# Two-block MetaFormer forward pass: tiles of dt and dt*u copied from SBUF to SBUF, and the instruction order made in several passes

## The chip, the cores and the metric

The kernel runs on one core of a Trainium2 chip. A core has five instruction queues: PE (TensorE, matmuls), DVE (VectorE), ACT (ScalarE), POOL (GpSimd) and SP (SyncE, which in this kernel issues every DMA transfer). Each queue works in the order in which its instructions were written and waits at an instruction until the semaphores that it names have come. The metric is the device time of one execution in microseconds; the time before is the median of three runs, 3570.58 us (3565.6 to 3573.31).

## The reference

The input is x (8, 384, 32, 32). Block 0 mixes with a Mamba state space over 1024 positions, block 1 with a displacement and a small Gaussian filter for 48 positions; each is followed by a feed-forward part with binarized weights and group-wise quantization (five of the eight batch entries take part; the others are left as zeros by the quantization). The part that the change touches is the state space:

```python
xc = conv1d(xin)                       # depthwise, 3 taps
u = silu(xc)
dbc = u @ x_proj_w.T                   # dt (24), B (16), C (16)
dt = softplus(dt @ dt_proj_w.T + dt_proj_b)
A = -exp(A_log)                        # (768, 16)
def step(h, (dt_t, B_t, C_t, u_t)):
    dA = exp(dt_t[..., None] * A)
    h = dA * h + (dt_t * u_t)[..., None] * B_t[:, None, :]
    y = einsum('bdn,bn->bd', h, C_t)
y = ys + u * D
out = (y * silu(z)) @ out_proj_w.T
```

There are 768 inner channels and 16 states for each; everything is float32.

## The kernel before

**Tiling.** The sequence of each batch entry is cut in two stretches of T = 512, so there are 16 units (b, s). The 768 channels are six blocks of 128 (JC = 6), j = 0 to 5. A scan step works on one unit, one block j and one group g of states (NG = 4 groups of four states). In SBUF a tile has 128 partitions. dt and dt*u come out of softplus and of a product as soft tiles with one channel in each partition. The scan wants another layout: 32 channels (D = 32) times four states (Q = 4) fill the 128 partitions, and each quarter of 32 partitions must hold the same 32 channels. So every block of 32 channels is needed four times, once in each quarter. This is what spread does: for one soft tile it fills two dts (or dus) tiles of [128, 2, 512], tile p with channel blocks 2p and 2p+1, four copies of each.

**prep and spread.** prep makes two blocks at a time: PE forms dt (L873), ACT applies softplus (L883), POOL multiplies by u (L896), and spread is called for dt (into dts) and for dt*u (into dus). A spread first writes the soft tile to a DRAM tile via (256 KB) and then issues eight reads of it, each into 32 partitions of a dts or dus tile with two channel blocks (128 KB). There are 192 spreads. The rings are: soft three slots, via twelve, dts four, dus four.

**scan.** For each (unit, j, g) and each half p: POOL multiplies dus by B (L927), ACT takes exp of dts times A twice (L937), DVE runs the recurrence with two scans (L952). For half 0 POOL multiplies by C (L973), for half 1 DVE does (L986). The last states are kept by POOL (L969) and ACT (L979). PE sums over states into y (L994). t tiles have five slots, and PE's sum gives them back. B and C reach the partitions through bc tiles, read from DRAM (bcd).

**Beside it.** The same queues carry the input and output projections (L704, L1056), the feed-forward parts (L1445 and L1524 on PE, L1457 and L1536 on ACT, gelu L1500 on ACT, clips on POOL), layer norms, and the displacement. Their weights come in by DMA for each use (w<-w1d, w<-w2d, win, wo).

**What sets the order.** Every instruction is first recorded as an Op with an engine, a supposed duration and a key (a place in the order, counted in scan steps). Flow.run then plays through a list schedule: at each moment a free engine takes, among its instructions whose inputs are there and whose tile slots are free, the one with the lowest key. The keys are shifted by pseudo-random amounts: DRAWS has one seed for each 25 us of planned time, and shift turns it into a shift by instruction (ONE) and by engine and kind (ALL). PEN is added to the key of an ACT instruction that needs another function table. SP is taken to issue in 0.38 us with at most eight transfers in flight (LANES), and the semaphores of its transfers are eight as well: every transfer waits for the eighth before it. The instructions are emitted in the order in which this play took them. So a change of one transfer's size or number changes the order of all five queues.

Of the kernel before, what the change touches and what calls it, by code (L numbers as in the profile page):

```python
# [17 lines left out]
P = 128  # L18
B, C, HW = 8, 384, 1024
T = 512  # L20
# [6 lines left out]
Q = 4  # L27
D = P // Q
# [21 lines left out]
PEN = 8.61  # L50
# [38 lines left out]

STEP = 25.0
DRAWS = [
    2588809238, 452375479, 3182300674, 892127437, 3031607106, 4190915799, 210801287, 2528267595,
    1456515859, 0, 3667191977, 1777003549, 0, 289602391, 2360043521, 2893761654,
    1734824177, 2595276797, 1859152535, 420106053, 3187747945, 3121993781, 3537900339, 3781817979,
    1783676794, 500156423, 1014657074, 812403421, 2779270353, 2511900677, 4161990074, 2234806154,
    3075364087, 332485381, 1936396653, 2423255391, 3223520118, 2106840927, 1194216589, 154361651,
    1325576476, 2228588731, 1746166578, 1393485667, 3298820094, 2167670678, 0, 1658737982,
    2077953505, 2037467793, 1520888315, 1581728111, 3672070717, 3354909891, 1803808393, 4150367721,  # L100
    3281395725, 1519460387, 901569797, 618278083, 3122266317, 2079668595, 1489438893, 4286922582,
    1437111022, 872287307, 1167138051, 0, 1838008287, 3016755925, 3498114163, 3916969487,
    180074838, 64412836, 507811054, 1600843621, 25363757, 0, 682985741, 3258605221,
    1225562961, 0, 2191594738, 2731506639, 0, 2590361159, 2105546166, 1917697076,
    2936522859, 449918706, 807634013, 1769699081, 4123052838, 3422563802, 2854028781, 3998098897,
    1351550483, 2957050150, 3108490381, 0, 3870246271, 3129552247, 4423401, 1585339085,
    2919941273, 2106441706, 2263314457, 1450830237, 318771235, 2472105454, 2452787799, 3820223235,
    1566145129, 2085494553, 835678459, 1114623705, 693252553, 4024613474, 833387989, 3847970403,
    1743556437, 2448629961, 1025051962, 888405083, 4144082655, 1523794525, 2137060207, 1893166927,
    3205541950, 693684995, 2577056702, 4001291010, 934710037, 2114703579, 3848563781, 3766732577,  # L110
]
ONE, ALL = (0.0, 2.0, 6.0, 16.0), (0.0, 6.0, 20.0, 60.0)
ENGS = ("PE", "DVE", "ACT", "POOL", "SP")


# [7 lines left out]
def drawn(a, b):  # L123
    return mixed((mixed(a) + b) & 0xFFFFFFFF) / 4294967296.0 - 0.5


def shift(seed, o):
    if not seed:
        return 0.0
    v = 0.0  # L130
    if seed & 3:
        v += ONE[seed & 3] * drawn(seed, o.n + 100)
    if seed >> 2 & 3:
        v += ALL[seed >> 2 & 3] * drawn(seed, ENGS.index(o.eng) + 5 * o.kind)
    return v


# [42 lines left out]


class Op:
    __slots__ = ("eng", "us", "lag", "fn", "bufs", "key", "n", "wait", "next", "table", "at", "ready", "kind")


SETS = {
# [10 lines left out]
TIE = 0  # L197
# [5 lines left out]
class Flow:  # L203
# [89 lines left out]
            last = ends[o.n]  # L293
        return fills

    def run(self):
        nc = self.nc
        waiting = {e: [] for e in self.on}
        busy = {e: 0.0 for e in self.on}
        table, now, out = None, 0.0, []  # L300
# [4 lines left out]
        ends = {}  # L305
        left = len(self.ops)
        step = 0
        draw = lambda k: DRAWS[k] if k < len(DRAWS) else 0

        def enter(o):  # L310

            new = {}
            for b in o.bufs:
                if b.slot is None and b.ring.ordered:
                    k = new[b.ring] = new.get(b.ring, 0) + 1
                    if b.n > b.ring.given + k - 1:
                        b.ring.turn.setdefault(b.n - k + 1, []).append(o)
                        return
            insort(waiting[o.eng], (o.key + shift(draw(step), o), o.n, o))

        for o in self.ops:
            if o.wait == 0:
# [2 lines left out]
        while left:  # L325
            if int(now / STEP) != step:
                step = int(now / STEP)
                for q in waiting.values():
                    q[:] = sorted((o.key + shift(draw(step), o), n, o) for _, n, o in q)
            while done and done[0][0] <= now + 1e-9:  # L330
                _, _, o = heapq.heappop(done)
                for p in o.next:
                    p.wait -= 1
                    if p.wait == 0:
                        p.ready = now
                        enter(p)
                for b in o.bufs:
                    b.left -= 1
                    if b.left == 0:
                        b.ring.free.append(b.slot)  # L340
                        b.end = now
            moved = False
            nexts = []
            for e, q in waiting.items():
                if busy[e] > now + 1e-9:
                    continue
                best = None
                for i, (k, n, o) in enumerate(q):
                    if best is not None and (k > best[0] or TIE and k == best[0]):
                        break  # L350
                    if o.table is not None and o.table != table:
                        t = o.ready + (self.HOLD[o.table] if o.key > RUSH else 0.0)
                        if now < t - 1e-9:
                            nexts.append(t)
                            continue
                        k += PEN
                        if best is not None and k >= best[0]:
                            continue
                    if e == "SP" and landed[-LANES] > now + 1e-9:
                        nexts.append(landed[-LANES])  # L360
                        break
                    if Ring.open(o.bufs):
                        best = (k, i)
                if best is None:
                    continue
                o = q.pop(best[1])[2]
                for b in o.bufs:
                    if b.slot is None:
                        b.slot = b.ring.free.pop(0)
                        b.ring.given += 1  # L370
                        for p in b.ring.turn.pop(b.ring.given, ()):
                            enter(p)
                us = o.us
                if o.table is not None and o.table != table:
                    us += self.SWITCH
                    table = o.table
                if e == "PE":
                    if now - idle >= IDLE:
                        cold = now + COLD
                    if now < cold - 1e-9:  # L380
                        us *= 2
                    if o.us > 0.5:
                        idle = now + us
                busy[e] = now + us
                if e == "SP":
                    dma_free = max(dma_free, now) + (o.lag - 1.8)
                    end = max(dma_free, now + us) + 1.8
                    landed.append(end)
                else:
                    end = now + us + o.lag  # L390
                heapq.heappush(done, (end, o.n, o))
                o.at = now
                if e == "PE":
                    ends[o.n] = now + us
                    for b in o.bufs:
                        b.at = min(b.at, now)
                out.append(o)
                left -= 1
                moved = True
            if moved:  # L400
                continue
            t = [x for x in busy.values() if x > now + 1e-9] + nexts
            if done:
                t.append(done[0][0])
            t = [x for x in t if x > now + 1e-9]
            assert t, "the instructions that are left wait for one another"
            now = min(t)
        self.end = now
        fills = self.gaps(out, ends) if self.filler else {}
        table = None  # L410
        out.sort(key=lambda o: o is not self.lead)
# [9 lines left out]
def metaformer_flow(ctx, tc, x, mw, f0, offset, f1, out):  # L421
# [77 lines left out]
    lt_r = ring("lt", [P, 4, P], 3)  # L499
    sm_r = ring("sm", [P, 16], 8, ordered=False)  # L500
    bcd_r = ring("bcd", [2 * N, T], 2, dr)
    via_r = ring("via", [P, T], 12, dr)
    hd_r = ring("hd", [NS * MC // 2, P, 2, T], 2, dr)
    x1 = [one(f"x1_{b}", [C, HW], NS * KC, dr) for b in range(B)]
    x2 = [one(f"x2_{b}", [C, HW], NS * KC, dr) for b in range(GS)]
# [339 lines left out]

    def spread(src, r):

        via = via_r.new()
        dma(lambda: via.ap, lambda: src.ap, [src], [via])
        dst = [r.new(Q), r.new(Q)]  # L850
        for p in range(2):
            for q in range(Q):
                dma(
                    lambda p=p, q=q: dst[p].ap[q * D : (q + 1) * D],
                    lambda p=p: via.ap.rearrange("(c d) t -> d c t", d=D)[:, 2 * p : 2 * p + 2, :],
                    [via],
                    [dst[p][q]],
                    128,
                )
        return dst  # L860

# [960 lines left out]
```

## Time and profile before

| What | Value |
|---|---|
| median of the runs, three of them | 3570.58 us |
| the profiled execution, its own time | 3572.66 us |
| its span | 3570.9 us |
| instructions in the profile | 35,878 |
| mean granted TensorE clock | 0.934 |
| bytes moved by DMA | 777.44 MB, 218 GB/s |
| share of the span in which the 16 DMA engines were busy | 75.4% |
| reads of via into dts and into dus | 768 and 768, of 128 KB |
| writes of via | 192, of 256 KB |
| SP's time from issue to landing, all transfers | 1.6 / 4.4 / 11.0 us (min / median / max) |

The busy share of an engine is an average over the whole span. An engine's idle time is put down to what ended it, and matmuls are pipelined, so a busy PE is not a PE at its peak. PEld is the loading of weights into the array, which overlaps with matmuls. A transfer's time to landing counts from SP's issue to the semaphore. The chain of waits is the sequence of work that ended last, followed back from the last instruction.

### The profile page before, as it was taken

What the parts mean: (1) busy time and instruction counts of PE and PEld (TensorE: products, weight loads), DVE (VectorE), ACT (ScalarE), POOL (GpSimd) and SP (SyncE); (2) the same over time, 40 slices, a digit from 0 to 9 for tenths busy, and PEclk for the clock granted to TensorE, in tenths of its full rate; (3) what the DMA queues carried; (4) which work ended last, traced back from release to release, by engine and by line L of the source; (5) the groups of instructions that cost most, each with busy time, mean ns of one, the idle gap of its engine ahead of it and who ended that gap; (6) DMA issues with size and microseconds to landing.
All of it is one profiled execution on the core that took longest, in us unless ns stands there. A gap on an engine that the chain in (4) does not pass through costs nothing.

```text
span 3570.9 us, 35878 instructions
## 1 busy us (share of the span) xinstructions
PE 3120.2 (87%) x9620; PEld 1136.4 (32%) x9620; DVE 3086.1 (86%) x3080; ACT 2469.2 (69%) x3641; POOL 3155.6 (88%) x1680
## 2 busy tenths in 40 slices
PE   5788888888899997899999789999878999877997
PEld 2222323223233332333333233333223333323334
DVE  2898988789887989998988999988898998889985
ACT  4777877757677686686768667777666777766561
POOL 3889999898797899889899997999989899998893
PEclk7888989998899998999999999999988999888999
DMA  6768768696775987769597686868777897977955
GB/s 156 185 185 229 213 199 224 176 249 183 222 221 166 271 243 205 203 200 253 178 270 235 180 233 213 247 193 265 228 205 241 237 254 224 275 209 221 267 171 178
DMA packets 680819, 777.44 MB, mean 218 GB/s; under 512 B 113688, under 2 KB 434088, under 8 KB 680616
## 3 DMA queue, kind: packets, MB, share of 16 engines
q1 hardware_dynamic: 680616, 775.14, 75.4%
q8 instruction: 77, 1.26, 0.2%
q14 instruction: 126, 1.03, 0.1%
HBM read 578.45 MB, written 196.48 MB: 217 GB/s over the span
## 4 chain that ended last, share of the span: by engine, by line
PE 37%; DVE 20%; DMA 12%; POOL 12%; ACT 10%; issue 7%; SPq 2%; POOLq 0%; DVEq 0%; ACTq 0%
PE mm L1445 11%; PE mm L1524 8%; POOL t L927 7%; DVE dp L952 6%; PE mm L704 5%; DVE t L952 5%; PE y L994 4%; PE mm L1056 4%; DVE t L986 3%; POOL t L973 2%; DMA dts<-via 2%; ACT L417 2%; ACT dp L937 2%; SPq L268 2%; DMA dus<-via 2%
## 5 line engine op out<-in xcount | busy, mean ns | idle before, releaser
L927 POOL TENSOR_TENSOR t<-dus,bc 128x1024 f32<-128x1024 f32 x768 | 1798.6, 2361 | 154.1 <-PE y L994 112.7
L973 POOL TENSOR_TENSOR t<-t,bc 128x1024 f32<-128x1024 f32 x384 | 905.6, 2361 | 57.1 <-DVE t L952 48.6
L1524 PE MATMUL mm<-hb,w 128*128 128x512 f32 x1440 | 679.6, 610 | 35.3 <-ACT hb L1500 15.5
L937 ACT ACTIVATE da<-dts,aneg 128x512 f32<-128x512 f32 x768 | 521.2, 685 | 254.4 <-DVE t L952 227.3
L1445 PE MATMUL mm<-tn,w 128*128 128x512 f32 x1440 | 663.1, 605 | 23.8 <-DMA w<-w1d 5.3
L937 ACT ACTIVATE dp<-dts,aneg 128x512 f32<-128x512 f32 x768 | 528.1, 688 | 182.5 <-DVE t L986 170.4
L994 PE MATMUL y<-t,sel 128*32 128x512 f32 x3072 | 531.4, 652 | 140.0 <-POOL t L973 79.6
L952 DVE TENSOR_TENSOR_SCAN dp<-dp,h,t 128x512 f32<-128x512 f32 x384 | 491.4, 1280 | 52.3 <-ACT dp L937 42.0
L952 DVE TENSOR_TENSOR_SCAN dp<-dp,t 128x512 f32<-128x512 f32 x384 | 468.4, 1220 | 69.9 <-ACT dp L937 49.2
L952 DVE TENSOR_TENSOR_SCAN t<-da,h,t 128x512 f32<-128x512 f32 x384 | 482.6, 1268 | 52.1 <-POOL t L927 45.5
L952 DVE TENSOR_TENSOR_SCAN t<-da,t 128x512 f32<-128x512 f32 x384 | 458.9, 1208 | 72.0 <-POOL t L927 58.7
L417 ACT ACT_TABLE_LOAD x372 | 477.3, 1283 | 6.2
L704 PE MATMUL mm<-xn,win 128*128 128x512 f32 x900 | 438.6, 629 | 42.0 <-DVE xn L595 9.9
L986 DVE TENSOR_TENSOR t<-dp,bc 128x1024 f32<-128x1024 f32 x384 | 465.9, 1213 | 8.2 <-ACT h L979 2.5
L1524 PEld LDWEIGHTS mm<-hb,w 128*128 128x128 f32 x1440 | 263.2, 192 | 441.5 <-issue 350.4
L1445 PEld LDWEIGHTS mm<-tn,w 128*128 128x128 f32 x1440 | 267.1, 192 | 409.8 <-issue 303.7
L1056 PE MATMUL mm<-z,wo 128*128 128x512 f32 x552 | 273.4, 626 | 5.9 <-DMA wo<-in_L_conv_out_proj_w 2.9
L704 PEld LDWEIGHTS mm<-xn,win 128*128 128x128 f32 x900 | 172.5, 199 | 293.1 <-issue 205.3
L1457 ACT ACTIVATE he<-mm,b 128x512 f32<-128x512 f32 x240 | 162.9, 680 | 126.0 <-PE mm L1445 124.9
L994 PEld LDWEIGHTS y<-t,sel 128*32 128x32 f32 x3072 | 80.1, 112 | 498.2 <-issue 168.9
L542 PE MATMUL mm<-sq,pick 96*128 96x512 f32 x208 | 129.7, 709 | 42.4 <-ACT sq L535 39.2
L1056 PEld LDWEIGHTS mm<-z,wo 128*128 128x128 f32 x552 | 103.6, 198 | 164.4 <-issue 143.5
(135 smaller groups left out, 3076.7 us busy)
## 6 DMA issues: line engine op xcount, KB each, us to landing
dts<-via SPq DMA_DIRECT2D x768, 128.0 KB, 4.0
dus<-via SPq DMA_DIRECT2D x768, 128.0 KB, 4.3
hd<-he SPq DMA_DIRECT2D x120, 512.0 KB, 4.7
hb<-hd SPq DMA_DIRECT2D x120, 512.0 KB, 5.8
via<-soft SPq DMA_DIRECT2D x192, 256.0 KB, 3.9
w<-w2d SPq DMA_DIRECT2D x120, 384.0 KB, 4.4
w<-w1d SPq DMA_DIRECT2D x240, 192.0 KB, 4.0
bc<-bcd SPq DMA_DIRECT2D x256, 128.0 KB, 5.0
```

The lines of the kernel that those rows point to most:

```text
L417: nc.scalar.preload_act_table_set(SETS[table])
L704: e.matmul(acc.ap, w.ap[:, k, :], xn.ap[:, k, :], start=(k == 0), stop=(k == KC - 1))
L927: lambda e, t=t, du=du: e.tensor_mul(t.ap, du.ap, wide(0)),
L937: lambda e, c=c, r=r, dt=dt: e.activation(decay(c), dt.ap[:, r, :], AF.Exp, scale=aneg.ap[:, j * Q + c, g : g + 1],),
L952: e.tensor_tensor_scan(t.ap[:, r, :] if p == 0 else decay(c), decay(c), t.ap[:, r, :], 0.0 if s == 0 else hst[j][p].ap[:, g, r : r + 1], A ...
L973: op("POOL", 2.35, lambda e, t=t: e.tensor_mul(t.ap, t.ap, wide(1)), [bc], [t])
L986: lambda e, t=t: e.tensor_mul(t.ap, da[2].ap, wide(1)),
L994: e.matmul(y.ap[c * D : (c + 1) * D, :], sel.ap, ts[c // 2].ap[:, c % 2, :], start=(g == 0), stop=(g == NG - 1), tile_position=(0, c * D),)
L1056: e.matmul(o.ap, flat()[:, j, :], zs[j].ap, start=(j == 0), stop=(j == JC - 1))
L1445: e.matmul(acc.ap, w.ap[:, k, :], tn.ap[:, k, :], start=(k == 0), stop=(k == KC - 1),)
L1457: lambda e, he=he, r=r, m=m, acc=acc: e.activation(he.ap[:, r, :], acc.ap, AF.Identity, bias=b1.ap[:, m : m + 1]),
L1524: e.matmul(acc.ap, w.ap[:, part * 2 + r, :], hs[m // 2].ap[:, r * T : (r + 1) * T], start=(m == 0), stop=(m == MC - 1),)
```

## The change

spread no longer goes through DRAM. It issues sixteen copies from the soft tile: for each of the four channel blocks c and each quarter q, 32 partitions of the soft tile go to 32 partitions of dts or dus (64 KB). A dts or dus tile now has eight parts, each written by its own copy. The ring via is gone.

The order is played through eight times instead of once. The first play uses the keys as before, with new seeds; every later play ranks an instruction by the time at which the play before it started it (divided by PACE), with seeds of its own and smaller shifts. The last play's order is emitted. Other constants (ROWS, CONVS, the K values, PEN, GBS) stay as they are.

```diff
-STEP = 25.0
+STEP, PACE = 25.0, 9.06
 DRAWS = [
...
 ]
-ONE, ALL = (0.0, 2.0, 6.0, 16.0), (0.0, 6.0, 20.0, 60.0)
+ONE = ((0.0, 2.0, 6.0, 16.0), (0.0, 0.3, 1.0, 3.0))
+ALL = ((0.0, 6.0, 20.0, 60.0), (0.0, 1.0, 4.0, 12.0))
...
-def shift(seed, o):
+def shift(seed, o, later):
...
-        v += ONE[seed & 3] * drawn(seed, o.n + 100)
+        v += ONE[later][seed & 3] * drawn(seed, o.n + 100)
     if seed >> 2 & 3:
-        v += ALL[seed >> 2 & 3] * drawn(seed, ENGS.index(o.eng) + 5 * o.kind)
+        v += ALL[later][seed >> 2 & 3] * drawn(seed, ENGS.index(o.eng) + 5 * o.kind)
...
-    def run(self):
-        nc = self.nc
+    def arrange(self, k):
+
+        draws = DRAWS[k]
...
-            insort(waiting[o.eng], (o.key + shift(draw(step), o), o.n, o))
+            insort(waiting[o.eng], (o.rank + shift(draw(step), o, k > 0), o.n, o))
...
         self.end = now
+        return out, ends
+
+    def run(self):
+        nc = self.nc
+        bufs = {b for o in self.ops for b in o.bufs}
+        for o in self.ops:
+            o.rank = o.key
+        for k in range(len(DRAWS)):
+            waits, lefts = [o.wait for o in self.ops], [(b, b.left) for b in bufs]
+            frees = [(r, list(r.free)) for r in {b.ring for b in bufs}]
+            out, ends = self.arrange(k)
+            if k + 1 == len(DRAWS):
+                break
+            for o, w in zip(self.ops, waits):
+                o.rank, o.wait = o.at / PACE, w
+            for b, left in lefts:
+                b.left, b.slot, b.at, b.end = left, None, 1e9, 1e9
+            for r, free in frees:
+                r.free, r.given, r.turn = free, 0, {}
         fills = self.gaps(out, ends) if self.filler else {}
...
-    via_r = ring("via", [P, T], 12, dr)
...
     def spread(src, r):
 
-        via = via_r.new()
-        dma(lambda: via.ap, lambda: src.ap, [src], [via])
-        dst = [r.new(Q), r.new(Q)]
-        for p in range(2):
+        dst = [r.new(2 * Q), r.new(2 * Q)]
+        for c in range(Q):
             for q in range(Q):
                 dma(
-                    lambda p=p, q=q: dst[p].ap[q * D : (q + 1) * D],
-                    lambda p=p: via.ap.rearrange("(c d) t -> d c t", d=D)[:, 2 * p : 2 * p + 2, :],
-                    [via],
-                    [dst[p][q]],
-                    128,
+                    lambda c=c, q=q: dst[c // 2].ap[q * D : (q + 1) * D, c % 2, :],
+                    lambda c=c: src.ap[c * D : (c + 1) * D, :],
+                    [src],
+                    [dst[c // 2][q * 2 + c % 2]],
+                    64,
                 )
         return dst
```

## The prediction

> **What bounds the kernel now.** I read the busy shares first, then the same three engines by stage.
>
> ```profile
> PE 3120.2 (87%) x9620; PEld 1136.4 (32%) x9620; DVE 3086.1 (86%) x3080; ACT 2469.2 (69%) x3641; POOL 3155.6 (88%) x1680
> ```
> ```profile
> 0.00:100.00 100.00, 61.76 (x162) 26.30 (x163) 33.16 (x39) 49.46 (x78) 41.04 (x44) 0.73 0.67 160
> 100.00:3450.00 3350.00, 2958.91 (x9097) 1061.53 (x9096) 2976.30 (x2949) 2377.36 (x3510) 3054.36 (x1608) 0.94 0.77 221
> 3450.00:3571.00 121.00, 99.50 (x363) 48.58 (x361) 76.64 (x95) 42.42 (x53) 60.17 (x29) 0.95 0.55 179
> ```
>
> The columns of the second fence are the stretch, its length, busy time of PE, PEld, DVE, ACT and POOL, the granted clock, the DMA share and GB/s. No engine is alone at its limit: PE, DVE and POOL stand within two points of each other, and in the middle stretch POOL, the fullest, still idles 3350.0 - 3054.4 = 295.6 us. That idle time, plus a start and an end in which the pipeline fills and drains, is all that transfers and order can win without less work. Next: who ends it.
>
> ```profile
> POOL t L927 <- PE y L994: 112.7, 72, 6.2
> POOL h L969 <- DVE t L952: 60.6, 28, 6.3
> POOL t L973 <- DVE t L952: 48.6, 21, 6.0
> POOL t L927 <- DMA dus<-via: 6.5, 3, 5.1
> ```
>
> (us in total, times, longest.) POOL mostly waits for a free t tile, which PE's sum at L994 gives back, and for DVE's scans. The transfers that the change rebuilds end 6.5 us of it. Over all engines, the tile view of via lists 33.0 us of waits on its transfers (its ten rows added); the largest are these.
>
> ```profile
>   ACT da L937: 14.0, 6
>   POOL t L927: 7.4, 4
> ```
>
> The chain of waits sees more of them. Adding all of its pieces by name, dts<-via has 17 pieces with 72.6 us, dus<-via 14 with 59.3, via<-soft 5 with 18.9: 150.8 us, 4% of the span. A typical place, start and length in us:
>
> ```profile
> 1801.03 3.79 DMA dts<-via
> 1804.84 4.53 DMA dus<-via
> 1809.38 4.19 DMA dts<-via
> ```
>
> The pieces follow one another on SP's queue: each is released by an earlier transfer, not by compute. The chain steps through whatever came last, so its share is an upper figure and the engines' own idle time (33.0 us) a lower one.
>
> **The change, part by part.** Prices of transfers, from issues (KB, median us to landing) and from SP's own line (ns min/median/max):
>
> ```profile
> dts<-via SPq DMA_DIRECT2D x768, 128.0 KB, 4.0
> via<-soft SPq DMA_DIRECT2D x192, 256.0 KB, 3.9
> bcd<-dbc SPq DMA_DIRECT2D x16, 64.0 KB, 2.8
> ```
> ```profile
> L268 SPq DMA_DIRECT2D dts<-via x768: 302/425/1665, 62.1 to 3430.4; - x192
> L268 SPq DMA_DIRECT2D bcd<-dbc x16: 332/338/532, 51.6 to 3226.4; - x16
> ```
>
> *Transfers.* There are 192 spreads (16 units, 6 channel blocks, dt and dt*u). Each had one 256 KB write and eight 128 KB reads; it now has sixteen 64 KB copies. Bytes fall from 192 x 1.25 MiB to 192 x 1 MiB. No row shows SBUF to SBUF; the nearest is the 64 KB bcd<-dbc, 2.8 us, and I take that (the other end is 4.0, the landing of today's reads). Delivery of one dt alone: today 0.37 + 3.9 + 8 x 0.425 + 4.0 = 11.7 us; then 16 x 0.338 + 2.8 = 8.2. For dt and dt*u together: today 2 x 0.37 + 3.9 + 16 x 0.425 + 4.0 = 15.4; then 32 x 0.338 + 2.8 = 13.6. So the leg through DRAM goes, but most of it is paid back in issues. On the chain this would be 18.9 us of via and 31 pieces x (131.9/31 - 2.8) = 45 us, together -64. By the engines' idle time it is at most -33. I take -33, because engines at 87% refill what one queue gives back; the ends are -64 and, if landing stays at 4.0 us, -10 (about half of the via pieces, as other queue work takes their place). What is late next is POOL's wait for t tiles (112.7 us), which this part does not touch.
>
> *SP's queue.* It issues 3,434 transfers now and 4,778 in the changed kernel's order: +1344, at 0.338 us = 454 us of queue time. Its 1928 us of waits (all rows of SP's own list added) are the cover: it is an in-order queue that mostly waits for a slot to come free. Of the 3,434 issues, 197 pieces with 66.8 us lie on the chain; the same share of the new ones is 66.8 x 1344/3434 x 0.338/0.425 = +21 us. Behind them stand the weight loads (w<-w1d, w<-w2d, win), for which PE's L1445, L1524 and L704 wait, the hd writes and reads of the FFN, and bc<-bcd for POOL. If the cover is gone it costs up to 454 us. Every transfer waits for the eighth before it: at 2.8 us to landing that passes one each 0.35 us, no tighter than the issue itself; at 4.0 it passes one each 0.5 us.
>
> *Waits per reader.* A half of dts or dus is now written by eight copies instead of four. In the two orders, waits on transfers grow from 892 to 1,349 on ACT and from 1,016 to 1,360 on POOL; each that does not fit the instruction is a semaphore instruction of 38 to 42 ns (medians at L937 and L927). That is up to 344 x 0.042 = +14 us on POOL. The page puts POOLq and ACTq at 0% of the chain, so I take +4; ends 0 and +14. Behind such a wait on ACT stand the FFN's evictions (L1457, L1536), and behind those PE's mm slots.
>
> *The soft tile* is held until sixteen copies have landed, 8.2 us instead of 0.37 + 3.9. Three slots serve four tiles of a prep, so the fourth (POOL L896) waits for the first one's copies. I cost it at nothing: a channel block lasts 3571/96 = 37 us, and L896 waited 0.5 us in all for via. Without this cover it would be 48 preps x 3.9 = 187 us. The DRAM ring's twelve parking places, which let a block be prepared before its dts slot is free, go as well; the same 37 us cover that.
>
> *The order.* All five queues are listed anew, every DMA of SP's and every compute instruction included; their numbers of instructions are the same but for SP's and for ACT's table loads, 376 in the listing of before and 353 in that of after.
>
> ```profile
> L417 ACT ACT_TABLE_LOAD x372 | 477.3, 1283 | 6.2
> ```
>
> That is 23 x 1.283 = 29.5 us less on ACT, which idles 973 us in the middle stretch. On the chain are 54 loads with 64.5 us, 14%; so -5 us (ends 0 and -29.5). What the rest of a new order is worth no row shows. Its stake is POOL's 295.6 us; I take the same 6% by which the loads fall, -18 us, and as ends a third of the stake won (-98) and a fifth lost (+59).
>
> Sum: -33 + 21 + 4 - 5 - 18 = -31. From the profiled span 3570.9, that gives 3540 us; span and median of the runs (3570.58) agree to 0.3 us, so nothing is added.
>
> A rule speaks against the first part. The row first: with 32-partition writes, dts<-via leaves each 0.425 us, 131 KB / 0.425 = 308 GB/s, because transfers overlap. The Trainium skill, "SBUF — State Buffer", section "Summary: rules for kernel authors", asks for 128 partitions and one transfer rather than several; "DMA: Bandwidth & Descriptors", section "Measured (HBM→SBUF, 128 partitions, SWDGE, issued from GpSimd)", puts a lone 64 KB transfer at 138 GB/s. By that rate an estimate is 201 MB / 138 GB/s = 1459 us for the spreads alone, and the sum would go to the slower rival. The row already goes past such a rate, so I stay with it.
>
> **The rivals.**
>
> *SP's queue becomes the bound (slower).* Place: the burst of a block, 32 copies where 18 stood, in front of weight loads. Price: 454 us of added queue time times the uncovered share. With the other terms at -52 (33 + 5 + 18 - 4), it decides from 52/454 = 11% uncovered, against the 5% (21 us) that I take. At 20% it is +91 - 52 = +39: 3610 us. For it: the queue's waits and its issues (3434 x about 0.4 = 1370 us) already fill 3300 us of the span, so there is no empty time, only waits that can shrink. Against it: most of SP's waits are for slots of weights whose readers hardly wait for them (PE L1445 waits 5.3 us for w<-w1d).
>
> *The order is worth much more (faster).* A third of POOL's idle time instead of 6%: 3540 - 80 = 3460 us. For it: 112.7 us of POOL's waits are for PE's L994, which an order can place earlier. Against it: three engines at 87% jam one another whichever goes first.
>
> *Hidden anyway (no change).* Transfers hide behind compute, and the order gives and takes: 3571 us. For it: only 33 us of engine waits name these transfers. Against it: all five queues differ from the first rows on, and a tie is unlikely.
>
> **How the numbers follow.** My forecast near 3540 has 0.43, the stronger gain 0.15, no change 0.07, the bound queue 0.35. No change means within 0.2%, 7 us, about what a measurement of this kernel can tell; its runs span 3565.6 to 3573.3. So faster 0.58, same 0.07, slower 0.35. The forecast's own range is 3507 (transfers at -64) to 3563 (transfers at -10). For 8 in 10 it reaches down to the stronger gain, 3460, and up past the slower rival, to 3620 (22% uncovered); 0.08 is left below and 0.12 above.
>
> **What would show it.** Right: dts<-soft lands in about 2.8 us with an issue near 0.34; ACT's and POOL's waits on dts and dus under 20 us; SP's waits shrink by about 400 us while PE's waits on w<-w1d, w<-w2d and win grow by under 20; table loads near 350; POOL's idle time in the middle near 265 us. Wrong: landing at 4 us or issues over 0.4 us, weight loads among the first releasers of PE, or POOL's idle time above 300 us for reasons of order (L994, L952) with the transfers in time.

## The result and the profile after

The changed kernel takes 3993.65 us (median of four runs, 3988.5 to 3996.92) against 3570.05 us for the kernel before: ratio 1.118, 95% interval 1.116 to 1.120. It is slower by 424 us. The prediction, 3540 us, had the wrong sign, and its range ended at 3620.

The page's busy line and the middle stretch of the changed kernel (stretch, length, busy time of PE, PEld, DVE, ACT, POOL, granted clock, DMA share, GB/s):

```profile
PE 3225.1 (81%) x9620; PEld 1171.2 (29%) x9620; DVE 3094.7 (78%) x3080; ACT 2440.1 (61%) x3618; POOL 3156.0 (79%) x1680
```
```profile
100.00:3850.00 3750.00, 3056.13 (x9048) 1096.20 (x9046) 2955.96 (x2924) 2339.64 (x3473) 3028.03 (x1596) 0.90 0.63 184
```

POOL and DVE do the same work as before (3155.6 and 3086.1 us then) in a longer span; PE's is 105 us longer at a lower granted clock (0.895 over the span, 0.934 before). In the later runs the clock is lower where the time is longer, whatever slowed the kernel (0.937 at 3520 us in half_copies; 0.900 at 3905 us in stale_before, which has the old transfers); what part of the 424 us it adds was not separated. POOL idles 3750.0 - 3028.0 = 722 us in the middle, against 296 before. DMA is not what filled up: its share fell from 0.77 to 0.63. The waits of the changed kernel (us in total, times, longest) show where it waits now:

```profile
POOL t L1071 <- PE y L1138: 314.1, 123, 11.1
PE mm L1589 <- DMA w<-w1d: 90.6, 33, 9.3
PE mm L1668 <- DMA w<-w2d: 70.2, 25, 7.6
ACT da L1081 <- DMA dts<-soft: 67.1, 16, 10.8
POOL soft L1040 <- DMA dts<-soft: 66.7, 15, 16.4
PE mm L850 <- DMA win<-in_L_conv_in_proj_w: 65.7, 21, 7.9
```

(L1071, L1138, L1589, L1668, L1081, L1040 and L850 are L927, L994, L1445, L1524, L937, L896 and L704 of before.) Weight loads, which PE hardly waited for, now stop it; the same rows before:

```profile
PE mm L704 <- DMA win<-in_L_conv_in_proj_w: 8.5, 5, 2.7
PE mm L1524 <- DMA w<-w2d: 7.5, 7, 2.1
PE mm L1445 <- DMA w<-w1d: 5.3, 7, 1.6
```

POOL's largest wait, 314 us, is for the t slots that PE's sum gives back (112.7 us before). Adding all rows whose releaser is a transfer, PE's idle time behind transfers rose from 61 to 384 us, POOL's from 44 to 276, ACT's from 30 to 117, DVE's from 38 to 100. Yet the transfers themselves land sooner than before (KB, median us to landing):

```profile
dts<-soft SPq DMA_DIRECT2D x1536, 64.0 KB, 2.2
dus<-soft SPq DMA_DIRECT2D x1536, 64.0 KB, 2.1
```

The weight loads land sooner too (w<-w1d 3.3 us, 4.0 before). So the transfers are late at their start. SP's own line in the changed kernel (ns, min/median/max):

```profile
L395 SPq DMA_DIRECT2D dts<-soft x1536: 507/588/3821, 53.1 to 3881.6; - x192
L395 SPq DMA_DIRECT2D dus<-soft x1536: 507/588/2199, 55.8 to 3880.4; - x192
L395 SPq DMA_DIRECT2D w<-w1d x240: 359/488/2055, 486.6 to 3803.4; - x120
```

A copy from SBUF to SBUF holds SP for 588 ns, where the prediction had 338. Loads issued among them cost more as well: w<-w1d has 488 ns, 376 before. SP's waits add up to 1140 us, 1928 before. What is not wait is 3992 - 1140 = 2852 us, against 3571 - 1928 = 1643: SP's work grew by about 1210 us. The lengths of SP's transfer issues, added up over the trace, say the same: 2660 us, 1469 before. A stretch of SP's timeline in the changed kernel (start, length in us) shows how a weight load gets lost in it:

```profile
2015.01 0.51 SPq L395 DMA_DIRECT2D dts<-soft  x1
2015.62 0.54 SPq L395 DMA_DIRECT2D w<-w2d  x1
2016.21 3.74 SPq L395 DMA_DIRECT2D dts<-soft  x6
2020.05 0.53 SPq L395 DMA_DIRECT2D w<-w1d  x1
2020.62 1.79 SPq L395 DMA_DIRECT2D dts<-soft  x3
2022.51 1.00 SPq L395 DMA_DIRECT2D bc<-bcd  x2
2023.56 1.78 SPq L395 DMA_DIRECT2D dts<-soft  x3
2025.44 6.87 SPq L395 DMA_DIRECT2D dus<-soft  x11
...
2066.48 1.84 SPq L395 DMA_DIRECT2D w<-w1d  x2
```

From 2015 to 2068 us SP has hardly a gap. Between the load of w1d at 2020.05 and the next at 2066.48 it issues 53 copies and 16 loads of bc, and no weights. PE does one load's worth of L1589 (six matmuls) in 2.7 us. After 2032 us it runs none, until the next load has landed (in brackets the idle time before, and what ended it):

```profile
2071.38 4.54 PE L1589 MATMUL mm<-tn,w 128*128 128x512 f32 x5 [9.32 <-DMA w<-w1d]
```

### The profile page after: what moved, and what is told of

Same layout as the page of the kernel before. It is cut to its first block, busy times and chain, and to the rows that moved or that the text cites. A ratio compares the mean times of both kernels' runs of the same rounds, so it can differ in the third digit from the quotient of the medians.

```text
span 3992.2 us, 37566 instructions
## 1 busy us (share of the span) xinstructions
PE 3225.1 (81%) x9620; PEld 1171.2 (29%) x9620; DVE 3094.7 (78%) x3080; ACT 2440.1 (61%) x3618; POOL 3156.0 (79%) x1680
## 5 line engine op out<-in xcount | busy, mean ns | idle before, releaser
L1071 POOL TENSOR_TENSOR t<-dus,bc 128x1024 f32<-128x1024 f32 x768 | 1797.3, 2357 | 423.0 <-PE y L1138 314.1
L1589 PE MATMUL mm<-tn,w 128*128 128x512 f32 x1440 | 714.0, 640 | 113.7 <-DMA w<-w1d 90.6
L1668 PE MATMUL mm<-hb,w 128*128 128x512 f32 x1440 | 708.3, 632 | 87.3 <-DMA w<-w2d 70.2
L1081 ACT ACTIVATE da<-dts,aneg 128x512 f32<-128x512 f32 x768 | 522.8, 685 | 353.4 <-DVE t L1096 277.6
L1081 ACT ACTIVATE dp<-dts,aneg 128x512 f32<-128x512 f32 x768 | 527.6, 687 | 183.0 <-DVE t L1130 153.4
L1138 PE MATMUL y<-t,sel 128*32 128x512 f32 x3072 | 517.4, 647 | 135.2 <-POOL t L1117 68.0
L850 PE MATMUL mm<-xn,win 128*128 128x512 f32 x900 | 445.4, 637 | 92.3 <-DMA win<-in_L_conv_in_proj_w 65.7
L1589 PEld LDWEIGHTS mm<-tn,w 128*128 128x128 f32 x1440 | 279.1, 202 | 537.2 <-issue 390.9
L1668 PEld LDWEIGHTS mm<-hb,w 128*128 128x128 f32 x1440 | 274.1, 199 | 509.9 <-issue 383.0
L1200 PE MATMUL mm<-z,wo 128*128 128x512 f32 x552 | 290.4, 663 | 40.7 <-DMA wo<-in_L_conv_out_proj_w 31.7
L850 PEld LDWEIGHTS mm<-xn,win 128*128 128x128 f32 x900 | 176.0, 202 | 348.6 <-issue 235.6
L1040 POOL TENSOR_TENSOR soft<-soft,u 128x512 f32<-128x512 f32 x96 | 121.9, 1270 | 153.0 <-DMA dts<-soft 66.7
L1138 PEld LDWEIGHTS y<-t,sel 128*32 128x32 f32 x3072 | 77.3, 112 | 483.1 <-issue 205.4
L1611 DVE TENSOR_REDUCE sm<-he 128x1 f32<-128x1024 f32 x120 | 144.4, 1204 | 66.4 <-ACT he L1601 64.8
```

The lines of the kernel that those rows point to most:

```text
L850: e.matmul(acc.ap, w.ap[:, k, :], xn.ap[:, k, :], start=(k == 0), stop=(k == KC - 1))
L1071: lambda e, t=t, du=du: e.tensor_mul(t.ap, du.ap, wide(0)),
L1081: lambda e, c=c, r=r, dt=dt: e.activation(decay(c), dt.ap[:, r, :], AF.Exp, scale=aneg.ap[:, j * Q + c, g : g + 1],),
L1138: e.matmul(y.ap[c * D : (c + 1) * D, :], sel.ap, ts[c // 2].ap[:, c % 2, :], start=(g == 0), stop=(g == NG - 1), tile_position=(0, c * D),)
L1200: e.matmul(o.ap, flat()[:, j, :], zs[j].ap, start=(j == 0), stop=(j == JC - 1))
L1589: e.matmul(acc.ap, w.ap[:, k, :], tn.ap[:, k, :], start=(k == 0), stop=(k == KC - 1),)
```

## The experiments

Theory A: the issue of these copies fills SP's queue. Theory B: the eight-pass order is at fault. Theory C: 64 KB transfers of 32 partitions move slowly.

**The price by itself.** The kernel issue_prices has SP issue 32 transfers of each of twelve shapes, nothing else on the chip:

```diff
+group("aa", cut(0, 32, T), own(0, 32, T), [128, T])             # SBUF to SBUF, 32 rows of 2 KB
+group("ai", cut(0, 32, T), lambda: x[0][0:32, :T], [128, T])    # DRAM to SBUF, the same shape
+group("ak", cut(0, 32, T), own(0, 32, T), [128, T], dr)         # SBUF to DRAM, the same shape
...
```

> Leaves out all of the computation: SP issues 32 transfers of each of twelve shapes, one shape after the other, with nothing else on the chip, and the output is filled from one tile. Theory A1 (the issue of a copy from SBUF to SBUF of 32 partitions costs SP 0.5 to 0.6 us by itself): aa and ab 0.5 to 0.6 us, a read from DRAM (ai) and a write to DRAM (ak) of the same shape 0.30 to 0.35. Theory A2 (the price comes from contention with the kernel's other transfers): aa and ab 0.30 to 0.40 us like ai and ak. If the price goes with the rows, ad (128 partitions) is far above aa and ag (16) below; if with the bytes, af (4 KB rows) is above aa and ae (512 B rows) below.

The tile view of the groups in issue_prices (ns, min/median/max; first and last start):

```profile
L25 SPq DMA_DIRECT2D aa<-src x32: 578/589/603, 3.0 to 22.7; - x32
...
L25 SPq DMA_DIRECT2D ad<-src x32: 598/630/652, 64.5 to 85.2; - x32
...
L25 SPq DMA_DIRECT2D ae<-src x32: 588/589/632, 85.9 to 105.6; - x32
...
L25 SPq DMA_DIRECT2D af<-src x32: 588/590/663, 106.2 to 126.3; - x32
...
L25 SPq DMA_DIRECT2D ag<-src x32: 507/587/735, 127.0 to 147.0; - x32
...
L25 SPq DMA_DIRECT2D ai<-in_x x32: 419/419/724, 168.5 to 183.4; - x32
...
L25 SPq DMA_DIRECT2D ak<-src x32: 302/422/540, 207.7 to 223.7; - x32
```

A1 is right about the copies: 589 ns on an idle chip, with no contention. With both ends in SBUF the price is nearly the same whatever is moved: 16 KB (ae), 64 KB (aa), 128 KB (af) and 256 KB (ad, 128 partitions, 630 ns), 16 rows instead of 32 (ag), aligned or shifted partitions (ab, 589 ns) all cost about the same. With one end in DRAM, 32 rows cost 419 to 422 in a row of such transfers, so the expected 300 to 350 was missed. It was met where the issues did not follow close on one another. The same view of parts of two groups (aj reads 128 rows from DRAM):

```profile
L25 SPq DMA_DIRECT2D aj<-in_x x10: 422/430/652, 183.8 to 188.3; - x10
L25 SPq DMA_DIRECT2D aj<-in_x x22: 327/328/373, 190.5 to 207.1; - x22
L25 SPq DMA_DIRECT2D ak<-src x7: 302/302/332, 207.7 to 211.6; - x7
```

The ten of the first line start every 0.5 us, one right behind another; the 22 of the second have pauses of at least 0.27 us before them, in which SP waits for a landing, and so have the seven of ak. So the price depends on the two ends, and on whether a transfer is issued right behind another. Sixteen small copies pay sixteen prices, where one larger copy would pay one.

**Half the bytes, half the count.** All three kernels keep the changed kernel's order on PE, DVE, ACT and POOL. From the ninth spread on, half_bytes moves only the first 256 columns of each copy; half_copies leaves out the copies for two of the four quarters, and twelve_copies those for one. What is not copied stays at old values.

```diff
+W = T if len(made) <= 8 else T // 2          # half_bytes
-lambda c=c: src.ap[c * D : (c + 1) * D, :],
+lambda c=c, W=W: src.ap[c * D : (c + 1) * D, :W],
...
+if q >= 2 and not full:                      # half_copies; q >= 3 in twelve_copies
+    o.fn = lambda e: None
```

> The changed kernel in its own order; from the ninth spread on each of the sixteen copies moves half of its columns (32 KB), so dt and dt*u are wrong in the other half. Theory A (the issue sets the time, and its price does not go with the bytes): issue stays 0.59 us and the time within 1.5% of the changed kernel, 3930 to 4050 us. Theory C (transfers of 32 partitions are slow to move): half of 200 MB less, under 3850 us.

> The changed kernel in its own order on PE, DVE, ACT and POOL; from the ninth spread on eight of its sixteen copies are not issued, so the upper half of the partitions of dts and dus holds old values. Same copy size, half the count: SP has 1,472 issues of 0.59 us less, 868 us. Theory A: 3500 to 3700 us, most of the loss gone. Theory B (the order itself is at fault): above 3850 us.

> As half_copies, but twelve of the sixteen copies are issued (the last quarter of the partitions holds old values). The plan reserved 16 x 0.38 = 6.1 us of SP for a spread; eight copies take 4.7, twelve 7.1, sixteen 9.4. Theory A, with a loss that starts where the real time passes the reserved one: 3600 to 3760 us, above the straight half of the way's lower side. If the loss were a plain sum in copies, half of the way between 3520 and 3993: 3757 us.

half_bytes took 3968 us (ratio 1.110, 1.103 to 1.117): with half the bytes nothing but 25 us goes, as theory A had it and against theory C. half_copies took 3520 us (ratio 0.985, 0.979 to 0.991), 474 us less than the changed kernel and under the kernel before: against theory B. Its waits for transfers are back near the old ones (PE 73 us, POOL 50; 61 and 44 before). Its busy line:

```profile
PE 3096.6 (88%) x9620; PEld 1134.3 (32%) x9620; DVE 3082.6 (88%) x3080; ACT 2438.2 (69%) x3618; POOL 3156.8 (90%) x1680
```

twelve_copies took 3637 us (ratio 1.019, 1.016 to 1.021). The first four copies more cost 117 us, the next four 357. The list schedule reserved 16 x 0.38 = 6.1 us of SP for a spread; eight copies take 8 x 0.588 = 4.7, twelve 7.1, sixteen 9.4. The loss grows faster than the count, as theory A has it (a plain sum would have given 3757). Three points don't tell where it starts, nor whether the reserved time or a full queue sets that place.

**The same transfers, cheaper to issue.** copies_from_dram keeps number, size and destination of the copies but reads the matrix w_in in DRAM, so dt and dt*u are those numbers, and a soft tile is free without waiting for copies.

```diff
-lambda c=c: src.ap[c * D : (c + 1) * D, :],
+lambda c=c: w_in[c * D : (c + 1) * D, :T],
```

> The changed kernel in its own order; the sixteen transfers of each spread keep number, size and destination but read a matrix in DRAM instead of the soft tile, so dt and dt*u are wrong, and a soft tile is free without waiting for them. Issue falls from 0.59 to 0.42 us by the price list, 3072 x 0.17 = 520 us of SP's time. Theory A: 3600 to 3830 us. Theory C (32 partitions, 64 KB): above 3930 us. The wait for soft tiles (136 us in the changed kernel) goes too, so a fall of up to 136 us alone would speak for that hold.

It took 3637 us (ratio 1.017, 1.011 to 1.023), 357 us less than the changed kernel. SP's line in copies_from_dram:

```profile
L395 SPq DMA_DIRECT2D dts<-in_L_conv_in_proj_w x1536: 310/419/2999, 53.1 to 3520.6; - x192
```

588 - 419 = 169 ns on 3,072 issues are 519 us of SP's time. The soft tiles, whose hold made POOL's L1040 wait 122 us for copies in the changed kernel, are freed by the same edit, and their hold was not tried alone. But twelve_copies, where the hold is left in, takes the same 3637 us with about the same work on SP. Five kernels have the changed kernel's order on the four engines and copies without a leg through DRAM; sorted by SP's work (span less SP's waits, in us) they are sorted by time, whatever the copies' number, size and source:

| Kernel | SP's work | Time |
|---|---|---|
| half_copies | 1873 | 3520 |
| copies_from_dram | 2324 | 3637 |
| twelve_copies | 2362 | 3637 |
| half_bytes | 2841 | 3968 |
| the changed kernel | 2852 | 3994 |

**The order.** Four kernels take spread and order apart. The no_seeds pair has one pass and all seeds zero, through DRAM and direct:

```diff
-DRAWS = [
...
+DRAWS = [0]
```

> The kernel before with all seeds zero: one pass, order by the keys alone. This is the base for no_seeds_direct, so that neither kernel has seeds that fit it. Both theories expect it slower than before, by 2 to 10%: 3640 to 3930 us.

> The same with the direct spread, nothing else: one pass, all seeds zero. Theory A: 300 to 500 us above no_seeds_via, with issues of 0.59 us. Theory B: within 100 us of it.

They took 3693 us (as expected) and 4313 us: the direct spread alone costs 620 us in an order fitted to neither, more than the 300 to 500 of theory A, and its PE waits 438 us behind transfers (68 in the other). Then the changed kernel's passes with the old spread put back, its control, and the passes without seeds:

```diff
 DRAWS = [ ... ]                              # via_new_order: the eight lists as they are
+via_r = ring("via", [P, T], 12, dr)
...
-v += ONE[seed & 3] * drawn(seed, o.n + 100)  # stale_before: the kernel before
+v += ONE[seed & 3] * drawn(seed, o.n + 101)
...
+DRAWS = [[0]] * 8                            # no_seeds_via_eight
```

> The changed kernel with the spread through DRAM put back (one 256 KB write and eight 128 KB reads), the order still made in eight passes; the seeds were drawn for another number of instructions, so some of their fit is lost. Theory A (SP's queue: a copy from SBUF to SBUF takes SP 588 ns to issue, so 3,072 of them fill it): 3560 to 3640 us, issue of dts<-via near 0.43 us, SP's waits back near 1900 us. Theory B (the eight-pass order is itself bad): 3850 to 4000 us.

> The kernel before with its seeds drawn for other instructions (the number of each is shifted by one); nothing else. It is the control for via_new_order, whose seeds had lost their fit too. If lost fit explains its 3948 us, this one is far above no_seeds_via: 3750 to 3950 us. If the eight passes explain it, this one stays at 3650 to 3720.

> The spread through DRAM, eight passes, all seeds zero: against no_seeds_via (3693 us, one pass) it shows what the passes do without seeds. If repeated passes improve the order by themselves: 3550 to 3670 us. If they do nothing: 3670 to 3730. If they spoil it: above 3750.

via_new_order took 3948 us (ratio 1.105), where theory A had 3560 to 3640. Most of that is not the passes: stale_before, the old kernel with seeds that fall on the wrong instructions, took 3905 us (ratio 1.094), 212 us above no seeds at all. Passes without seeds gave 3744 us, 50 us above one pass and between the expectations for doing nothing and for harm. In these two kernels seeds that have lost their list of instructions do harm. So the time of via_new_order says nothing about theory A. Its waits do: its PE waits 78 us behind transfers, against 384 in the changed kernel at nearly the same time.

**The planner.** planner_told corrects the plan's price of a copy:

```diff
-def dma(self, dst, src, reads=(), writes=(), kb=256.0):
+def dma(self, dst, src, reads=(), writes=(), kb=256.0, us=0.38):
...
                     64,
+                    0.59,
```

> The changed kernel with one constant of the list schedule corrected: a copy from SBUF to SBUF keeps SP for 0.59 us instead of 0.38. The seeds stay, so they fit less. Theory A1 (the work on SP is too much wherever it is put): 3850 to 4050 us. Theory A2 (the loss comes from a plan that did not know the price): under 3750 us.

It took 4334 us (ratio 1.212), outside both expectations, and near no_seeds_direct. That its seeds had lost their fit too is likely and not shown. Whether a plan that knows the price and has seeds found for it could hide the copies stays open.

**The old transfers in the new order.** These three compute everything and keep the changed kernel's list of instructions, and so its order on the four engines. The sixteen places of a spread on SP carry one write to DRAM and eight reads of 128 KB. In via_in_its_slots each read stands at the second of its two places; in reads_later and reads_latest it is put on the queue at least 4 or 8 planned us after the write (or right ahead of the first instruction that needs it).

```diff
+if not seen:
+    e.dma_start(via, src.ap)
+if (p, q) in seen:
+    e.dma_start(dst[p].ap[q * D : (q + 1) * D], via.rearrange(...)[:, 2 * p : 2 * p + 2, :])
+seen.add((p, q))
...
+fl.pending.append((wrote[0] + LATER, dst[p], read))     # LATER 4.0 or 8.0
```

> The changed kernel with the order of PE, DVE, ACT and POOL exactly as it is; only on SP the sixteen copies of a spread become, at their own places, one write of the soft tile to DRAM and eight reads of 128 KB, each at the second of the two places that it stands for. SP's spread costs 0.37 + 8 x 0.42 = 3.8 us instead of 16 x 0.59 = 9.4, but SP waits for the write to land before the first read. Theory A (SP's issue is the whole loss, the new order is better than the old): 3500 to 3580 us, at or under the kernel before. Theory B (the new order is no better): 3580 to 3700 us.

> As via_in_its_slots, but a read of the DRAM tile is put on SP's queue no sooner than 4 planned us after its write (or right ahead of the first instruction that needs it). SP then issues other transfers while the write lands. If SP's stand of 490 us made the 3643 us: 3490 to 3560 us, under the kernel before, SP's waits for via under 200 us. If the order is no better than the old one: 3580 to 3650 us.

> The same with 8 planned us. SP's waits for via under 50 us. If the stand made the time: 3480 to 3560 us, at or under reads_later, unless the later reads make ACT and POOL wait for dts and dus (then above reads_later). If the order: 3580 to 3650 us.

via_in_its_slots took 3643 us (ratio 1.020, 1.018 to 1.022): 351 us of the 424 come back, but the time lies in theory B's range (an order no better than the old one) and above theory A's. SP's wait for the write in it (its largest), in reads_later and in reads_latest:

```profile
SPq L1005 <- DMA via<-soft: 489.9, 165, 6.9
```
```profile
SPq L1016 <- DMA via<-soft: 258.9, 111, 6.7
```
```profile
SPq L1016 <- DMA via<-soft: 63.8, 36, 5.6
```

reads_later took 3574 us (ratio 1.001, 0.9997 to 1.0023), reads_latest 3584 us (1.004, 1.002 to 1.005). With SP's stand before unlanded writes halved, 69 of the 73 us over the kernel before are gone, so it made most of them. But the hoped-for 3490 to 3560 was missed: taking away more of the stand did not go below the kernel before, and with 8 us other work waits (ACT da on dts<-via 29.7 us against 23.5 with 4 us, POOL t on bc<-bcd 30.3 against 17.1). So with the transfers of before, the new order takes the time of the old one, and the direct copies make the loss of 420 us. A gain from the order does not show. None that computes everything beats the kernel before.

## Why the prediction was wrong

**The step that failed is SP's price.** The prediction took the issue of a copy from the row of bcd<-dbc, 0.338 us, because it is the nearest in size; it is a write to DRAM, and the price goes with the two ends, not with the bytes. The 3,072 copies cost 3072 x 0.588 = 1806 us of SP where the 1,728 old transfers cost 1536 x 0.425 + 192 x 0.372 = 724: +1082 us, not +454. With the dearer issue of the loads between them SP's work grew by about 1210 us. The prediction also priced only the 1,344 added issues, though all 3,072 are of the new kind. And the row's median was no bound: 13 of its sixteen issues came after a pause, and ak shows 302 ns for such ones against 422 in a row. That error is the smaller one: at 422 ns the copies would have cost 3072 x 0.422 - 724 = +572 us.

**The mechanism of the slower rival was right, its size was not.** "SP's queue becomes the bound" had the place (a block's burst in front of weight loads), the sign that would show it (weight loads among PE's first releasers) and the condition (more than 11% uncovered). Its price was 454 us, of which 20% gave 3610. Measured, about 424 of 1210 us are uncovered, 35% (taking the other terms as nothing, as none of their gains shows). It was right that SP's queue has "no empty time, only waits that can shrink": the waits shrank by 788 us, and the rest became span. Two of its own signs of being wrong came: issues over 0.4 us, and weight loads among the first releasers of PE. (The lower end of its range, 3507, is a slip: 3540 less 31 is 3509.)

**Transfers (-33).** They land in 2.1 to 2.2 us, sooner than the 2.8 assumed, and the leg through DRAM is gone. It won nothing, as the queue ahead of them grew: ACT waits 86 us for dts and POOL's L1071 43 us for dus, not under 20.

**The soft tile, costed at nothing.** The cover was a block's 37 us. It failed with SP: POOL's L1040 waited 153 us in all, 122 of them for copies of a soft tile. A copy's tile is held for about 16 x 0.588 + 2.1 = 11.5 us even if nothing comes between, not 8.2, so most of the hold is issue time. Its own share was not tried apart from the issue's; that copies_from_dram, without it, is no faster than twelve_copies speaks for a small one.

**Table loads (-5) and waits per reader (+4).** ACT's busy time fell by 2469.2 - 2440.1 = 29.1 us as worked out. Neither term shows in a time of its own.

**The order (-18).** No run shows a gain from it with all work done: reads_later is at 1.001. In half_copies, with fewer issues and 96 MB less to move, the same order gives 0.985; how much of that is the order's and how much the missing work's is open.

**The rule on small transfers** was set aside because a row of 128 KB reads already ran past its rate. The 64 KB copies do not: in issue_prices the group aa moves 97 GB/s, below the rule's 138, with the 16 DMA engines 40% busy. So the rule's sum pointed the right way, to the slower rival, though the limit is not the bytes (half_bytes) but the price of each issue. The Trainium skill, "DMA: Bandwidth & Descriptors", section "Issuing engines are not separate DMA queues", calls the time to initiate a transfer usually small relative to the transfer. Here it is 0.59 us of a 2.1 us transfer, and as the transfers of a burst overlap, it is the issue that repeats.

## What to carry to other kernels

Price a transfer first by what it costs the queue that issues it, and take that price from a row with the same two ends; size tells little. Look too whether that row's transfers stood alone or in a burst like yours. A queue that is never empty but mostly waits can take more work only so far: here 2340 us of it cost some 70 us over the kernel before, and 2850 us cost 424. Past that the loads behind are late, and PE, which waits most for them, uses none of the new transfers. The order found by seeds here belongs to one list of instructions, so an experiment on such a kernel should keep the list and change what an instruction does.

## What the hardware showed that was not expected

A transfer from SBUF to SBUF holds SP for 587 to 596 ns (medians) from 16 KB to 128 KB and 630 ns at 256 KB, in a row of its like, against 419 ns for 32 rows from DRAM and 422 to DRAM. After a pause each is cheaper. In the changed kernel's trace a copy took 507 ns (median) where at least 0.25 us lay before it and 589 right behind another; in copies_from_dram a read took 311 and 419. So the price goes with the two ends and with what was issued just before; why, no run tells. Other transfers issue more slowly behind such a copy as well: w<-w1d took 528 ns there and 365 after a pause of 0.6 us or more (medians in the changed kernel). At 256 KB something else comes in. Writes of 128 rows to DRAM (tile al, 431/642/650) begin at 431 to 454 ns and rise to about 642, and ad rises from 601 to about 643, while both groups move some 370 GB/s with the DMA engines busy all the time. That these hold up the issue is not shown. Bytes cost nearly nothing in the kernel's time: halving about 96% of the copies changed 3994 to 3968 us.
